# Layer 0's checks moved into bursts at the ends of rounds, and a new order in the first six pairs of the joint sums

## The chip, the cores and the metric

The kernel runs on one core of one Trainium2 chip. The core has five engines that run on their own queues and meet only at semaphores: TensorE (PE, matrix products into PSUM), VectorE (DVE), ScalarE (ACT), GpSimd (POOL) and SyncE (SP), which here only issues transfers. Transfers run on 16 DMA engines. The metric is the device time of one execution in microseconds; three runs of the kernel before took 573.9, 572.15 and 574.8 us, median 573.9.

## The reference, cut to what matters

Four graph layers follow each other on the same 4096 nodes with 64 features and one 4096 x 4096 adjacency matrix `adj` of zeros and ones:

```
h = relu(layernorm(x));  x = x + L0(h)   # att = adj * sigmoid(scores(q, k)); att @ h, normalised
h = relu(layernorm(x));  x = x + L1(h)   # weighted sum over the last 100 neighbours by rank, + bias
h = relu(layernorm(x));  x = x + L2(h)   # 1 - 0.1 h - 0.01 * rowsum(h * (adj @ h))
h = relu(layernorm(x));  x = x + L3(h)   # relu([h, adj @ h / degree] @ W.T)
```

Layer 0 needs a full 4096 x 4096 matrix of sigmoids, masked by `adj`, times a 4096 x 64 matrix. Layer 1 needs running counts of each row's neighbours. Layers 2 and 3 both need a product of `adj` with 64 columns, and are summed jointly in the kernel.

## The kernel before

`adj` stands in DRAM as f32, cut into 8 blocks `ib` of 512 rows and, in each block, 16 tiles `g` of 2 x 128 columns. GpSimd loads it once as FP8 masks that stay in SBUF (`load_masks`, L211). That is exact only where the entries are zeros and ones. So the kernel also reads `adj` again as f32 and lets VectorE test every entry; this is a check (`check`, L441 and L438 in its `fetch`). An accumulated count of odd entries goes into `odd`, and at the end a flag decides whether a general version of the model (`model(True)`) has to run. A check in layer 0 takes half a tile, 128 x 512 (tile `ck`, three buffers, `CHECKED`); later checks take a whole tile, 128 x 1024 (tile `ckw`, or free space of `s2a`). A check has no effect on the other work except that it takes VectorE's time, a transfer on SP's queue, and a buffer. `fetch` puts the transfer in front of its check in the program; SP runs ahead and issues it as soon as the buffer is free, that is when the check three before it has ended.

**Layer 0.** After a prologue up to about 58 us, the scores are made in rounds. A round has four tiles (the rounds of the first two blocks after the prologue's 18 tiles have 4, 4, 3 and 3), a block has four rounds. For each tile, TensorE makes the scores into one of three PSUM buffers of two banks (`scores`, L1059), ScalarE takes the sigmoid (`sigmoids`), and VectorE multiplies with the mask (`masked`). The first sigmoid of a round is written to SBUF and so frees its PSUM buffer by itself; the other three stay in PSUM, and VectorE's product frees the buffer. After the four tiles come, on TensorE, the sums with the four tiles of the round before (`gather`, L1090). When a block is complete, `rows0` is pushed onto a list of jobs: one part of it is emitted after each tile (`on`, which calls `step`). Its parts go TensorE (pt, L266), ScalarE, GpSimd (sup), ScalarE (sq), VectorE (inn, rs_y), GpSimd (a root by Newton steps, rs_a, then sup and x_sb), VectorE (st), GpSimd (xc), ScalarE (sq), VectorE (va, rs_y), GpSimd (the root again), VectorE (xc), GpSimd and VectorE (s2a, the input of layer 1). Each engine takes its instructions in the order in which the program emits them; no scheduler changes it (`manual_schedule`).

From the 33rd tile on, five of eight tiles are followed by a check, 60 in layer 0: after tiles with `k % 8` in (0, 2, 4, 5, 7), so one to three among the four products of a round. `taken`, between tile 84 and 112, issues copies of two mask rows per block on SP's queue (apart_m). If the number of checks left is odd after the loop, one more is made.

`Planned` wraps VectorE (`dve`) and ScalarE (`act`) and keeps a running estimate of when each will be done (`end`), from a cost of 0.07 us + 0.00105 us per column for VectorE. The planning of layer 1 uses it together with `clock`; in layer 0 `clock` stays at zero and nothing reads the estimates.

**Layer 1** first counts chunks (`many`), then runs rounds of four count products (L1500) and four sums (L1535), with checks by a plan: `due` grows in each round, and a check is made where the estimate says that VectorE is free.

**The joint sums** (`both_summed`) add up layers 2 and 3 for 32 tiles of 128 rows, in 16 pairs; a pair takes one PSUM bank, each tile 32 products over the chunks `t` (L1632), 1024 products in all. The last blocks of layer 1 are still being finished then by the jobs `rows1`: pr, then a norm, then ph (transposes, L1352), ht on ScalarE, pn (products, L1367), and the split into `s23`, which is what chunk `t` of the joint sums reads (`need` emits jobs until chunk `t` is ready). After every 8 products `beat` emits one part of each job, and every second beat a check. The first six pairs (`LEAD`) run side by side over the first 28 chunks (`SPLIT`): with `SKEW = 1`, pair `p` is `p` chunks behind pair 0. In `rows1` a number of empty parts stands in front of ph: 6 for blocks 6 and 7 (`late`), else 1; blocks 0 to 3 are `early`.

Of the kernel before, what the change touches and what calls it, by code (L numbers as in the profile page):

```python
# [28 lines left out]
IB = 512  # L29
# [49 lines left out]
def kernel(  # L79
# [87 lines left out]
    def model(general):  # L167
# [901 lines left out]
        def sigmoids(ps, to=None):  # L1069

            to = ps if to is None else to
            act.activation(to, ps, AF.Sigmoid, bias=att_c, scale=att_a)
            return to
# [119 lines left out]
        with tc.manual_schedule():  # L1193
            acc, late = first_rows_and_block()
            push(rows0(order0[0], evacuated(order0[0], acc, 0)), 10)
            pro_stack.close()
            mp1 = pool("mask_b", 1, side="right")
            for ib in order0[EARLY:]:
                get_mask(mp1, ib)
            spare.append(pool("pp1", 1, l0, space=PSUM))  # L1200
            if not general:
                push(count_constants(), 1)
            asking = iter(())

            def on():
                step()
                next(asking, None)

            sizes = [2] * 8 if general else [4] * 4
            first = [2] * 7 if general else [4, 4, 3, 3]
            sizes = first + (NIB - 2) * sizes + [0]
            k, done = NG + 2, NG
            LEAVING = {112 - 4 * ib: ib for ib in range(NIB)}
            for size in sizes:
                now = []
                for n, (ib, g) in enumerate(todo[k : k + size]):
                    edge[0] = n == size - 1
                    ps = scores(ib, g)  # L1220

                    if size > 2 and not now:
                        att = frm = sigmoids(ps, att_tile(ib, g))
                    else:
                        frm, att = sigmoids(ps), att_tile(ib, g)
                    masked(ib, g, frm, att)
                    now.append((ib, g, att))
                    load_masks(1)
                    k += 1
                    if k == 92 and not general:  # L1230
                        push(count_constants_2(), 1)
                    if not general and k in LEAVING:
                        taken(LEAVING[k])
                    if k > 2 * NG and k % 8 in (0, 2, 4, 5, 7):
                        check()
                    on()
                for ib, g, att in late:
                    at = done % NG
                    if at == 0:
                        acc = pa0.tile([P, IB], F32, tag="pa", name=f"acc0_{ib}{sfx}")  # L1240
                        if ib > 0:
                            asking = queries(ib - 1)
                    gather(acc, fb, g, att, at)
                    if at == NG - 1:
                        push(rows0(ib, evacuated(ib, acc, 0)), 10)
                    done += 1
                late = now
            edge[0] = True
            if len(checks) % 2:
                check()  # L1250
            if general:
                drain()
# [61 lines left out]
        def rows1(ib, asb):  # L1314
            tag = f"1_{ib}"
            rows = block(ib)
            xr = x_sb[:, rows, :]
            yield
            yield from claim("bank")
            pt = pm.tile([P, CI, D], F32, tag="pr", name=f"pr{tag}{sfx}")  # L1320
            for c in range(CI):
                nc.tensor.matmul(
                    pt[:, c, :], asb[:, c * P : (c + 1) * P], wln_sb[:, 0, :],
                    start=True, stop=True,
                )
            yield
            dve.tensor_tensor(xr, xr, pt, ALU.add)
            yield
            used.discard("bank")
            h = fa[:, rows, :]  # L1330
            if general:
                yield from norm(rows, h, tag, True)
                return
            early, late = ib < NIB - 4, ib >= NIB - 2
            yield from norm(rows, h, tag, True, kept=kept, pool=early)
            yield from split(h, s2b, rows)
            yield
            if early:
                nc.gpsimd.tensor_scalar(h, h, -0.1 / UP, None, ALU.mult)
                nc.gpsimd.tensor_tensor(h, h, xr, ALU.add)  # L1340
            else:
                dve.scalar_tensor_tensor(h, h, -0.1 / UP, xr, ALU.mult, ALU.add)
            yield
            scratch = s23[:, rows, 2:4, :].rearrange("p t k d -> p t (k d)").bitcast(F32)
            yield from norm(rows, h, f"3_{ib}", True, 1.0, late, h, sq=scratch, pool=early)
            for _ in range(6 if late else 1):
                yield
            yield from claim("rows")
            yield from claim("bank")
            pt = pm.tile([P, CI, P], F32, tag="pr", name=f"ph_{ib}")  # L1350
            for c in range(CI // 2):
                nc.tensor.transpose(  # L1352
                    pt[:, c, :], h[:, 2 * c : 2 * c + 2, :].rearrange("p c d -> p (c d)"), ident
                )
            yield
            ht = temps.tile([P, CI // 2, P], F32, tag="ht", name=f"ht_{ib}")
            act.copy(ht, pt[:, 0 : CI // 2, :])
            for _ in range(2 if late else 1):
                yield
            pn = [  # L1360
                pm.tile([P, CI // 2, 2, D], F32, tag="pr", name=f"pn_{ib}_0"),
                bank(turn_of_banks(), f"pn_{ib}_1", (P, CI // 2, 2, D)),
            ]
            v = temps.tile([P, CI, D], F32, tag="two", name=f"v2_{ib}")
            for c in range(CI):
                half = slice(c % 2 * D, (c % 2 + 1) * D)
                nc.tensor.matmul(  # L1367
                    pn[c % 2][:, c // 2, :, :].rearrange("p s d -> p (s d)"),
                    ht[half, c // 2, :],
                    wln_sb[half, 1:3, :].rearrange("p s d -> p (s d)"), start=True, stop=True,  # L1370
                )
            for n in (1, 0):
                act.copy(h[:, n::2, :], pn[n][:, :, 0, :])
                act.copy(v[:, n::2, :], pn[n][:, :, 1, :])
            yield
            used.discard("bank")
            yield from split(v, s23[:, :, 2:4, :], rows)
            used.discard("rows")
            ready.setdefault(2, set()).add(ib)
# [227 lines left out]
        if general:  # L1607
# [1 line left out]
            stream2 = pool("stream2", 2, l2)  # L1609
            own_sb = epi2.tile([P, NT, D], F32, name="own" + sfx)  # L1610
            v_sb3 = epi2.tile([P, NT, D], F32, name="v3" + sfx)
        SKEW = 1
        summed, beats = [0], [0]

        def beat():
# [296 lines left out]
```

## Time and profile before

One execution was profiled; its own time is 572.18 us, of which the recorded span is 569.5 us.

| | before |
|---|---|
| median of three runs | 573.9 us (572.15 to 574.8) |
| profiled execution, its span | 572.18 us, 569.5 us |
| granted TensorE clock, mean | 0.997 |
| busy: TensorE, VectorE, ScalarE, GpSimd | 552.0, 467.5, 358.8, 272.2 us |
| layer 0 after the prologue | 58 to 296 us |
| chunk counts, then layer 1 | 296 to 311 us, 311 to 444 us |
| joint sums | 444 to 563 us, the end at 569.5 |

Between 140 and 260 us VectorE is busy 36 to 37 us of every 40 and TensorE over 39 of 40; the 16 DMA engines are busy nearly all of the time there, most of it with the mask loads on GpSimd's queue, until about 250 us. From 482 to 556 us TensorE has no idle time.

How to read the rows: in a timeline the first number is the start in us from the span's start, the second the duration, then the engine, the line, the operation, the tile written and those read, and the count; brackets hold the idle time before the row and what ended it. In the list of waits the numbers are the total, the count and the longest. In the chain of waits each row is what held up the next one. L73 is the helper of `Planned`, so VectorE's and ScalarE's rows all carry it and are told apart by their tiles.

### The profile page before, as it was taken

What the parts mean: (1) busy time and instruction counts of PE and PEld (TensorE: products, weight loads), DVE (VectorE), ACT (ScalarE), POOL (GpSimd) and SP (SyncE); (2) the same over time, 40 slices, a digit from 0 to 9 for tenths busy, and PEclk for the clock granted to TensorE, in tenths of its full rate; (3) what the DMA queues carried; (4) which work ended last, traced back from release to release, by engine and by line L of the source; (5) the groups of instructions that cost most, each with busy time, mean ns of one, the idle gap of its engine ahead of it and who ended that gap; (6) DMA issues with size and microseconds to landing.
All of it is one profiled execution on the core that took longest, in us unless ns stands there. A gap on an engine that the chain in (4) does not pass through costs nothing.

```text
span 569.5 us, 9915 instructions
## 1 busy us (share of the span) xinstructions
PE 552.0 (97%) x3368; PEld 280.8 (49%) x3368; DVE 467.5 (82%) x949; ACT 358.8 (63%) x663; POOL 272.2 (48%) x526
## 2 busy tenths in 40 slices
PE   8999999999999999999999999999999999999995
PEld 3563333333333333333334444445454788888884
DVE  4679657799999999898976877778969897799993
ACT  3677667766676776778741888988888432342231
POOL 7624402675757576754444510384634343334332
PEclk9999999999999999999999999999999999999998
DMA  8995952689999999994223465453544788859960
GB/s 145 133 106 47 100 50 20 57 131 154 150 169 150 166 126 173 152 158 121 74 89 113 151 209 168 132 170 112 155 145 132 241 266 304 274 190 323 343 251 21
DMA packets 45612, 87.86 MB, mean 154 GB/s; under 512 B 6272, under 2 KB 24576, under 8 KB 45552
## 3 DMA queue, kind: packets, MB, share of 16 engines
q1 hardware_dynamic: 26112, 69.14, 36.5%
q0 software_dynamic: 18912, 17.77, 33.0%
q8 instruction: 28, 0.46, 0.3%
q10 hardware_dynamic: 528, 0.23, 0.2%
q14 instruction: 32, 0.26, 0.2%
HBM read 135.60 MB, written 1.05 MB: 240 GB/s over the span
## 4 chain that ended last, share of the span: by engine, by line
PE 70%; DVE 13%; POOL 5%; ACT 5%; issue 3%; DMA 2%; DVEq 0%; ACTq 0%; POOLq 0%; SPq 0%
PE acc L1090 15%; PE acc L1632 15%; PE ps L1059 15%; PE acc L1535 8%; PE cnt L1500 8%; PE idle L1183 3%; DVE att L73 3%; DVE ckw L73 2%; PE many L1387 1%; DMA s2a<-adjt_dram 1%; DVE s2a L73 1%; ACT ps L73 1%; DVE rrq L73 1%; POOL mask L211 1%; PE pt L266 1%
## 5 line engine op out<-in xcount | busy, mean ns | idle before, releaser
L1059 PE MATMUL ps<-qt,kt 64*128 64x512 f32 x512 | 123.4, 610 | 3.4 <-DVE att L73 3.0
L1090 PE MATMUL acc<-att,fb 128*64 128x512 f32 x512 | 117.8, 599 | 0.6 <-DVE att L73 0.5
L1632 PE MATMUL acc<-s,mask 128*128 128x256 f16 x1024 | 114.0, 273 | 0.4 <-DVE s L73 0.4
L73 ACT ACTIVATE w<-cnt 128x512 int16<-128x512 f32 x187 | 98.6, 606 | 12.1 <-PE cnt L1500 11.0
L1632 PEld LDWEIGHTS <-mask 128*128 128x128 fp8e4 x1024 | 99.8, 98 | 13.0 <-issue 1.0
L73 DVE TENSOR_TENSOR att<-ps,mask 128x1024 f32<-128x1024 f32 x82 | 98.6, 1217 | 8.6 <-ACT ps L73 8.5
L73 DVE SCALAR_TENSOR_TENSOR ckw<-ckw 128x1024 f32<-128x1024 f32 x76 | 96.0, 1274 | 4.2 <-DMA ckw<-adjt_dram 4.2
L73 ACT ACTIVATE ps<-ps,att_c,att_a 128x1024 f32<-128x1024 f32 x82 | 93.8, 1175 | 1.3 <-PE ps L1059 0.8
L73 ACT ACTIVATE att<-ps,att_c,att_a 128x1024 f32<-128x1024 f32 x46 | 54.6, 1202 | 54.1 <-PE ps L1059 53.9
L1059 PEld LDWEIGHTS ps<-qt,kt 64*128 64x128 f32 x512 | 44.8, 186 | 79.0 <-issue 28.7
L211 POOL DMA_DIRECT2D mask<-adjt_dram x128 | 70.1, 560 | 19.1 <-DMA mask<-adjt_dram 17.4
L73 DVE TENSOR_TENSOR att<-att,mask 128x1024 f32<-128x1024 f32 x46 | 56.9, 1252 | 18.8 <-ACT att L73 18.5
L1500 PE MATMUL cnt<-mask,after 128*128 128x512 fp8e4 x256 | 67.4, 379 | 2.7 <-DVE two L73 0.8
L1090 PEld LDWEIGHTS acc<-att,fb 128*64 128x64 f32 x512 | 33.5, 136 | 73.0 <-issue 67.6
L1535 PE MATMUL acc<-w,s2a 128*128 128x512 bf16 x256 | 66.2, 379 | 1.2 <-ACT asb L73 1.2
L73 DVE TENSOR_SCALAR w<-cnt 128x512 int16<-128x512 f32 x69 | 46.9, 686 | 22.6 <-PE cnt L1500 22.2
L301 POOL TENSOR_TENSOR rs_a<-rs_y 128x4 f32<-128x4 f32 x48 | 19.1, 398 | 67.4 <-DVE rs_y L73 61.0
L73 DVE SCALAR_TENSOR_TENSOR ck<-ck 128x512 f32<-128x512 f32 x60 | 42.8, 713 | 0.0
L1535 PEld LDWEIGHTS <-s2a 128*128 128x128 f16 x256 | 24.6, 98 | 33.6 <-issue 5.6
L1500 PEld LDWEIGHTS <-after 128*128 128x128 bf16 x256 | 24.4, 99 | 31.0 <-issue 2.7
L73 ACT ACTIVATE xm<-xm,inn 128x64 f32<-128x64 f32 x32 | 10.4, 347 | 45.9 <-DVE high L73 44.2
L1183 PE MATMUL idle<-ones 128*128 128x512 bf16 x126 | 30.9, 401 | 1.6 <-DVE ones L73 1.6
(248 smaller groups left out, 611.9 us busy)
## 6 DMA issues: line engine op xcount, KB each, us to landing
ckw<-adjt_dram SPq DMA_DIRECT2D x76, 512.0 KB, 4.3
mask<-adjt_dram POOLq DMA_DIRECT2D x128, 128.0 KB, 8.7
ck<-adjt_dram SPq DMA_DIRECT2D x60, 256.0 KB, 5.9
s2a<-adjt_dram SPq DMA_DIRECT2D x22, 512.0 KB, 4.9
x_sb<-x_dram SPq DMA_DIRECT2D x4, 256.0 KB, 7.5
out_dram<-y POOLq DMA_DIRECT2D x15, 64.0 KB, 3.7
apart_m<-mask SPq DMA_DIRECT2D x16, 16.0 KB, 4.1
mask<-apart_m SPq DMA_DIRECT2D x16, 16.0 KB, 4.3
```

Of the source, the lines that this page charges most:

```text
L73: return op(out, *args, **kw)
L211: nc.gpsimd.dma_start(out=masks[ib][:, g * CG : (g + 1) * CG, :], in_=adjt[ib, g])
L266: nc.tensor.transpose(pt[:, c, :], part, ident)
L301: nc.gpsimd.tensor_tensor(a, y, y, ALU.mult)
L1059: nc.tensor.matmul(ps[:, c, :], kt[half, g, :], qts[ib][half, :], start=True, stop=True)
L1090: nc.tensor.matmul(acc[c * D : (c + 1) * D, :], lhs[:, t, :], rhs[:, c, :], start=(at == 0), stop=(at == NG - 1), skip_group_check=True,)
L1183: nc.tensor.matmul(v.idle[:, v.filling % CG, :], ones, ones.unsqueeze(1).to_broadcast([P, IB // P, P]), start=True, stop=True, skip_group_ ...
L1387: nc.tensor.matmul(pc[q * NT : (q + 1) * NT, :], lane[:, NT - 1 - t : 2 * NT - 1 - t], masks[quad * QUAD + q][:, t, :], start=(t == 0), st ...
L1500: nc.tensor.matmul(cnt, by, what, start=True, stop=True, skip_group_check=True)
L1535: nc.tensor.matmul(accs[ib], apart_s if t < 0 else both(s2a, t), w, start=(t == NT - 1), stop=False, skip_group_check=True,)
L1632: nc.tensor.matmul(acc[:, to, :, :].rearrange("p k d -> p (k d)"), masks[ib][:, t, c * P : (c + 1) * P], s23[:, t, :, :].rearrange("p k d ...
```

## The change

Three places are touched. In layer 0 the check after a tile goes. Instead `clock` is set at the loop's start and grows by 7.7 for each round; a tile's product is planned no earlier than 2.1 + 1.2 n into its round; and after the products of a round, `due` grows by 2.5 (60 checks over 24 rounds) and checks are emitted while one is due and the plan says that VectorE would be done before the next round's first product, or three are due. The jobs of the round's tiles are emitted before the burst. As built, the bursts have 2 and 3 checks in turn, 60 in all as before.

In `rows1` the empty parts in front of ph become 5 for blocks 6 and 7, 3 for blocks 4 and 5, and stay 1 for blocks 0 to 3. `SKEW` becomes 0: the six pairs take each chunk together.

```diff
-            k, done = NG + 2, NG
+            k, done, due = NG + 2, NG, 0.0
+            TURN_0, FIRST_0, EACH_0, CHECKS_0 = 7.7, 2.1, 1.2, 60
+            clock[0] = max(dve.end, act.end)
...
+                    dve.end = max(dve.end, clock[0] + FIRST_0 + EACH_0 * n)
                     masked(ib, g, frm, att)
...
                     if not general and k in LEAVING:
                         taken(LEAVING[k])
-                    if k > 2 * NG and k % 8 in (0, 2, 4, 5, 7):
+                    on()
+                if k > 2 * NG and now:
+                    due += CHECKS_0 / (NIB - 2) / (NG / size)
+                    while due >= 1 and (
+                        dve.end + dve.cost(IB) < clock[0] + TURN_0 + FIRST_0 or due >= CHECKED
+                    ):
                         check()
-                    on()
+                        due -= 1
+                clock[0] += TURN_0
                 for ib, g, att in late:
...
-            for _ in range(6 if late else 1):
+            for _ in range(5 if late else 1 if early else 3):
                 yield
...
-        SKEW = 1
+        SKEW = 0
```

As built, the orders on TensorE and VectorE change where this says. Over layer 0 VectorE's row work keeps its place among the products, and a block reads, by VectorE's tiles: four products with va and rs_y before the last, two checks; two products, xc, two products, three checks; a product, s2a, three products, inn and rs_y, two checks; four products, st, three checks. On SP the apart_m copies stand up to three check transfers earlier. GpSimd's order is the same throughout, ScalarE's up to the joint sums.

## The prediction

> **What bounds the kernel now**
>
> Read in this order: the page, TensorE's waits, its timeline, the chain of work, VectorE's timeline beside it, and the landing of the checks' transfers. The page says that TensorE carries the kernel:
>
> ```profile
> span 569.5 us, 9915 instructions
> PE 552.0 (97%) x3368; PEld 280.8 (49%) x3368; DVE 467.5 (82%) x949; ACT 358.8 (63%) x663; POOL 272.2 (48%) x526
> ```
>
> Of the 17.5 us in which TensorE is idle, 3.3 lie in the first 60 us and 6.2 in the last 13.5 (windows); the change touches neither. Of its waits, these bear on the change, the first in layer 0, the others where the joint sums begin:
>
> ```profile
> PE ps L1059 <- DVE att L73: 3.0, 5, 0.8
> PE ph L1352 <- DVE x_sb L73: 0.5, 1, 0.5
> PE acc L1632 <- DVE s L73: 0.4, 1, 0.4
> ```
>
> Some loss hides in stretched rows. TensorE's timeline, start and duration first:
>
> ```profile
> 192.30 3.70 PE L1059 MATMUL ps<-qt,kt 64*128 64x512 f32 x16
> 195.93 3.65 PE L1090 MATMUL acc<-att,fb 128*64 128x512 f32 x16
> 199.52 3.92 PE L1059 MATMUL ps<-qt,kt 64*128 64x512 f32 x16
> 203.37 3.65 PE L1090 MATMUL acc<-att,fb 128*64 128x512 f32 x16
> 206.96 1.99 PE L1059 MATMUL ps<-qt,kt 64*128 64x512 f32 x8
> 209.56 1.99 PE L1059 MATMUL ps<-qt,kt 64*128 64x512 f32 x8 [0.62 <-DVE att L73]
> ```
>
> From start to start an undisturbed round is 3.63 of scores and 3.59 of sums. A round's third scores need the PSUM slot that the last product of the round before gives back, so that product's deadline is 1.83 us into the next round (half of 3.63 and the gap). It is missed once in a block of four rounds, and the chain of waits says why:
>
> ```profile
> 192.03 1.21 DVE att L73
> 195.13 1.05 POOL rs_a L301
> 199.65 1.09 POOL sup L1039
> 203.12 1.08 POOL mask L211 x2
> 205.20 1.17 ACT ps L73
> 206.39 1.22 DVE att L73
> 208.28 1.24 DVE att L73
> 209.56 1.99 PE ps L1059 x8
> ```
>
> VectorE reaches the row statistics late, so GpSimd's root and norm are late, ScalarE's square holds up the third sigmoid, and the last product misses its deadline. Checks stand in front of all this:
>
> ```profile
> 204.81 0.68 DVE L73 SCALAR_TENSOR_TENSOR ck<-ck 128x512 f32<-128x512 f32 x1
> 205.42 0.08 DVE L73 DVE_READ_ACCUMULATOR ck<-ck 128x1 f32 x1
> 206.39 1.22 DVE L73 TENSOR_TENSOR att<-ps,mask 128x1024 f32<-128x1024 f32 x1 [0.89 <-ACT ps L73]
> ```
>
> The answer on the tile ck says when a check's data is there, 5.9 us after the issue:
>
> ```profile
> DMA to landing us min/median/max: 2.6/5.9/7.9
> ```
>
> **The change, part by part**
>
> *What there is to win in layer 0.* In TensorE's timeline the four waits after the first check (178.62, 209.56, 240.88, 264.49) are 0.77, 0.62, 0.77 and 0.68: 2.84. Seven score rows (at 138.07, 145.60, 168.43, 199.52, 230.46, 237.90, 269.99) exceed 3.70, or 1.99 for half a row, by 0.20 to 0.32: 1.64. Together 4.48, the upper bound. The wait of 0.21 at 110.81 is before any check and stays.
>
> *The load.* Still 60 checks, 10 a block, now in bursts of 3 and 2 behind a round's products. VectorE's starts lie 1.14 apart behind a product and 0.61 behind a check; the row work of a block takes 1.11 (inn), 0.52 (st), 0.75 (va), 0.34 (xc) and 0.86 (s2a). So 16 x 1.14 + 10 x 0.61 + 3.58 = 27.9 us a block, against TensorE's 4 x 7.22 + 0.59 (pt) + 0.37 (pq) = 29.8. Starts of pt at 149.45, 180.54, 211.48, 242.80 and 273.82 give 30.9 to 31.3 now.
>
> *The new order by hand*, in the block shown. Third round: two checks no longer stand before inn, so the root's seed ends at 193.7, not 194.98, and GpSimd's chain begins 1.3 earlier. Fourth round: two checks to 194.9, then four products, the second at 197.3 behind its sigmoid; the last ends at 200.7. Deadline 199.52 + 1.83 = 201.35: the stretch of 0.22 goes. st to 201.2, three checks to 203.0. Next round: the first product starts at 203.0 (was 202.53), the third sigmoid ends 1.2 earlier, at 205.2; products at 203.0, 204.1 and 205.3, va to 207.2, the last product to 208.4, before the deadline of 208.79. The wait goes, with 0.2 to 0.4 to spare. Products here range from 1.21 to 1.64, so I leave 0.15 at each of five blocks: 0.75. Layer 0 gains 4.48 - 0.75 = 3.7; bounds 0 and 4.48, apart from late transfers.
>
> *The transfers, a new wait.* Three buffers: a check's transfer is issued when the check three before it ends. Today the tightest gap from issue to check is 6.6 us and no check waits (idle 0.0 in its group). In bursts, issues are 0.61 apart, and by the hand order the gap is 6.4 for the second check of a two-burst and the last of the three-burst behind it, 7.6 or more for most others. During mask loading, transfers issued 1.75 apart (179.20, 180.95) landed 2.1 apart by their packets (183.69, 185.79). So the second lands at 5.9 + 2.1 - 0.61 = 7.4, 1.0 late. Behind a waiting check stand the next round's four products, and behind these TensorE's scores; but that round's last product has 1.45 us to its deadline, and a block has 29.8 - 27.9 = 1.9 to spare. I take 0. From below the price is 0 (landing 5.9); from above, every queued transfer later than 7.4, priced in the third rival.
>
> The Trainium skill, "DMA: Bandwidth & Descriptors", section "Queues, rings and completion order", says that each DMA engine alternates between the queues that have work, one packet at a time. With GpSimd's mask queue always loaded, a check's transfer would move at half speed: 1.4 us alone (the transfer issued at 274.26 has packets from 0.95 to 2.31 us after its issue), so an estimated 2.8 instead of 2.1, the second landing 1.7 late, 0.25 over the slack, twice a block for 4.5 blocks: 2.2 less gain, and the sum would end at 571.6. The measured 2.1 decides.
>
> *Queues passed.* On SP the copies apart_m<-mask of the last block now stand before three check transfers instead of behind two of them; SP waited there until 258.64, so those start at 259.8 and land by 262.3 (2.5 without mask traffic), for a burst at 263.5. ScalarE and GpSimd keep their order, mask issues included. The final burst ends near 296.4 instead of 294.6; VectorE's next check waits for a transfer until 299.19. If its buffers come 0.4 later, wn_size is ready by 301.0, for TensorE at 301.20. Layer 1 keeps every engine's order and just moves.
>
> *Joint sums.* Same 1024 matmuls, 0.109 each start to start. Chunk 24 is first read after 288 instead of 258 of them, 3.3 us later, so the wait of 0.43 (a gap of 0.705, 0.60 over 0.109) goes. Block 5's transposes come 8 matmuls later, 0.87; what they wait for, x_sb at 457.61, ends at 458.02: 0.58 goes. Pair 5's bank is taken after 10 instead of 40 matmuls, at 445.2; its reader asb ends by 444.7. Block 6 goes the other way: its pn would start at 472.7, but ht ends at 472.95 on ScalarE, behind block 7's root, and a check (1.14) now stands before block 7's kept sum, which with VectorE's order costs some 0.2. A new wait of 0.4. Net 1.18 - 0.4 = 0.8; bounds 0 (that check delays all behind it) and 1.2. VectorE is busy 35.48 of 36 us from 520 to 556, but its run starts behind ScalarE's high at 489.32 after 1.57 idle and so moves along.
>
> *Sum.* -3.7 - 0.8 = -4.5. The profiled execution took 572.18 us (span 569.5 and 2.7 around it), so 567.7. It lies 1.7 below the median of the three runs, 573.9; against that, 569.4.
>
> **The rivals**
>
> 1. The forecast, 569.4; its own range 568 to 571.
> 2. GpSimd, not VectorE's checks, sets the third sigmoid: five mask issues (2.72 us) stand between x_sb and the norm whatever VectorE does. For it: its spans vary from 0.2 to 1.07 for the same rs_a. Against: the chain enters it from VectorE. Then the stretches go, the waits halve and the joint sums give 0.5: -1.6 - 0.5, 571.8.
> 3. Slower: bursts choke on their own transfers. VectorE's spare 1.9 us a block must be eaten first; beyond it each microsecond is TensorE's, over 4.5 blocks under mask loads. To end 2.9 above 573.9 it takes (4.5 + 2.9) / 4.5 = 1.65 more, 3.6 us of waiting a block: five queued transfers landing 0.7 beyond their gaps of 6.4 to 7.9, so at about 8 on average. Single ones reach 7.9 today, the median is 5.9. Then 577.
> 4. The wins are taken back, say by the flag's matmul at 556.05 waiting for VectorE, or late transfers that just use them up: 573.5.
>
> **How the numbers follow**
>
> Chances 0.62, 0.20, 0.12 and 0.06. A measurement of this kernel tells about 0.5% (2.9 us) from no change: the line is 571.0. Faster: the forecast and a little of rival 2, 0.66; same 0.22; slower 0.12. The range begins at both upper bounds off the lowest run, 572.15 - 4.48 - 1.2 = 566.4, and ends at 573.8, above rivals 2 and 4; what is out is rival 3 and a little.
>
> **What would show it**
>
> Right: TensorE's waits on att in layer 0 shrink from 3.0 to under 1.2, pt starts 29.8 to 30.1 apart, no DMA row before ck above 2 us in all, ph without its wait, pn with one below 0.5. Wrong: idle of ck <- DMA of 3 us a block, a third sigmoid still near 5.7 us into its round, or new waits past 460.

## The result, and where the time went

The changed kernel takes 575.64 us at the median of 17 runs (573.97 to 577.53), the kernel before 573.16 in the 17 runs beside it. The ratio is 1.0040, with a 95% interval of 1.0024 to 1.0056: 2.3 us slower. That is inside the band of 0.5% that the prediction counted as no change, but the interval leaves 1 out, so the small loss is real. The forecast was 569.4, its range 566.4 to 573.8. It missed, on the slow side.

The page of the profiled execution after the change (574.75 us, span 573.2) begins:

```profile
span 573.2 us, 9901 instructions
PE 551.2 (96%) x3356; PEld 280.7 (49%) x3368; DVE 472.2 (82%) x949; ACT 358.7 (63%) x663; POOL 267.1 (47%) x526
```

VectorE is 4.7 us busier than before, although it runs the same 949 instructions. TensorE's waits (us in total, times, longest) are now:

```profile
PE ps L1059 <- DVE att L73: 4.4, 8, 0.8
PE cnt L1509 <- DMA mask<-two: 1.5, 1, 1.5
PE pn L1376 <- ACT ht L73: 1.1, 1, 1.1
```

The first was to fall from 3.0 to under 1.2. The second was 0.4 before. The third is the new wait that the forecast put at 0.4; the waits of ph and of the joint sums' acc are gone, as it said. VectorE's own waits between 100 and 300 us begin with one that was not there at all before, the checks' wait for their transfers:

```profile
DVE ck L73 <- DMA ck<-adjt_dram: 6.8, 7, 1.4
DVE att L73 <- ACT att L73: 3.1, 4, 1.4
DVE att L73 <- ACT ps L73: 2.6, 5, 1.4
DVE st L73 <- POOL x_sb L1040: 2.2, 4, 0.7
```

And the checks themselves took longer. This is their group in the page of before, then in that of after (busy time, mean ns of one, idle time in front):

```profile
L73 DVE SCALAR_TENSOR_TENSOR ck<-ck 128x512 f32<-128x512 f32 x60 | 42.8, 713 | 0.0
```

```profile
L73 DVE SCALAR_TENSOR_TENSOR ck<-ck 128x512 f32<-128x512 f32 x60 | 44.7, 781 | 6.8 <-DMA ck<-adjt_dram 6.8
```

TensorE's timeline of the block that the prediction worked through has the missed deadline still in its place, with a second wait in front of it:

```profile
200.43 3.70 PE L1059 MATMUL ps<-qt,kt 64*128 64x512 f32 x16
204.06 3.65 PE L1090 MATMUL acc<-att,fb 128*64 128x512 f32 x16
208.04 2.26 PE L1059 MATMUL ps<-qt,kt 64*128 64x512 f32 x8 [0.32 <-DVE att L73]
211.07 1.99 PE L1059 MATMUL ps<-qt,kt 64*128 64x512 f32 x8 [0.77 <-DVE att L73]
```

The chain of work through this block no longer passes through GpSimd, ScalarE's sigmoid and their square. From the burst on it is VectorE alone:

```profile
204.29 1.02 DVE ck L73 x2
205.30 3.81 DVE att L73 x3
209.11 0.34 DVE va L73
...
209.79 1.24 DVE att L73
...
211.07 1.98 PE ps L1059 x7
```

VectorE's timeline of the same stretch, and GpSimd's row beside it, say what the burst met:

```profile
202.45 0.42 DVE L73 TENSOR_REDUCE st<-x_sb 128x4 f32<-128x256 f32 x1 [0.70 <-POOL x_sb L1040]
...
203.59 0.69 DVE L73 SCALAR_TENSOR_TENSOR ck<-ck 128x512 f32<-128x512 f32 x1
...
204.21 1.09 DVE L73 SCALAR_TENSOR_TENSOR ck<-ck 128x512 f32<-128x512 f32 x1
...
205.23 1.62 DVE L73 TENSOR_TENSOR att<-att,mask 128x1024 f32<-128x1024 f32 x1
...
209.79 1.23 DVE L73 TENSOR_TENSOR att<-ps,mask 128x1024 f32<-128x1024 f32 x1
```

```profile
205.06 0.70 POOL L332 TENSOR_TENSOR xc<-x_sb,st 128x256 f32<-128x256 f32 x1
```

st comes late, the three checks stand behind it, the third check (1.09, not 0.69) and the next product (1.62, not 1.22) run beside GpSimd's xc, and the round's last product ends at 211.02, 2.98 us into its round against a deadline of 1.83.

By stages: layer 0, from the first scores of the tenth tile (at 63.65 us before; the prologue's 18 tiles are scored until 79.6 us, not 58) to the first `many` matmul, takes 234.2 us instead of 232.2. The counting matmul behind it waits 1.1 longer for its transfer, and the joint sums, from their first to their last matmul, take 0.2 less. So the loss is in layer 0, where the gain was forecast.

### The profile page after: what moved, and what is told of

Same layout as the page of the kernel before. It is cut to its first block, busy times and chain, and to the rows that moved or that the text cites. A ratio compares the mean times of both kernels' runs of the same rounds, so it can differ in the third digit from the quotient of the medians.

```text
span 573.2 us, 9901 instructions
## 1 busy us (share of the span) xinstructions
PE 551.2 (96%) x3356; PEld 280.7 (49%) x3368; DVE 472.2 (82%) x949; ACT 358.7 (63%) x663; POOL 267.1 (47%) x526
## 4 chain that ended last, share of the span: by engine, by line
PE 65%; DVE 17%; ACT 5%; POOL 5%; DMA 4%; issue 3%; ACTq 0%; DVEq 0%; POOLq 0%; SPq 0%
PE acc L1641 15%; PE ps L1059 14%; PE acc L1090 13%; PE cnt L1509 8%; PE acc L1544 8%; DVE att L73 8%; PE many L1396 1%; DVE ckw L73 1%; DMA s2a<-adjt_dram 1%; DMA vec<-vecs_dram 1%; DMA mask<-adjt_dram 1%; ACT w L73 1%; DMA mask<-two 1%; PE idle L1183 1%; DVE rrq L73 1%
## 5 line engine op out<-in xcount | busy, mean ns | idle before, releaser
L73 DVE TENSOR_TENSOR att<-ps,mask 128x1024 f32<-128x1024 f32 x82 | 96.8, 1215 | 3.5 <-ACT ps L73 2.9
L73 DVE TENSOR_TENSOR att<-att,mask 128x1024 f32<-128x1024 f32 x46 | 59.4, 1306 | 15.1 <-ACT att L73 15.1
L1544 PE MATMUL acc<-w,s2a 128*128 128x512 bf16 x244 | 64.1, 379 | 1.8 <-ACT asb L73 1.2
L73 DVE SCALAR_TENSOR_TENSOR ck<-ck 128x512 f32<-128x512 f32 x60 | 44.7, 781 | 6.8 <-DMA ck<-adjt_dram 6.8
L301 POOL TENSOR_TENSOR rs_a<-rs_y 128x4 f32<-128x4 f32 x48 | 15.8, 330 | 70.7 <-DVE rs_y L73 64.3
```

Source lines behind the costliest of these rows:

```text
L73: return op(out, *args, **kw)
L301: nc.gpsimd.tensor_tensor(a, y, y, ALU.mult)
L1544: nc.tensor.matmul(accs[ib], apart_s if t < 0 else both(s2a, t), w, start=(t == NT - 1), stop=False, skip_group_check=True,)
```

## The experiments

Three theories were set against each other. *Theory 1*: the bursts wait for their own transfers. *Theory 2*: it is the order, a burst of three behind a late st and in front of the next round's first product. *Theory 3*: VectorE is full, because its rows beside GpSimd's cost more than the forecast charged.

Each run was timed beside the kernel before. In the table, "rows" is what VectorE's rows occupy in a block of four rounds: the mean length of five blocks (between the starts of pt) less the idle time that VectorE's timeline shows in front of its rows. The two waits are TensorE's on att and VectorE's on a check's transfer, in us, over the whole execution. These columns and layer 0 come from one profiled execution of each run. Runs with the same code in layer 0 show how far that can be trusted: before and joint alone differ by 0.1 us, the whole change and layer 0 alone by 0.5.

```
run                          ratio to before [95%]      layer 0   rows   att    ck
before                       1                          232.2     28.6   3.0    0
the whole change             1.0040 [1.0024, 1.0056]    234.2     29.4   4.4    6.8
layer 0 alone                1.0044 [1.0022, 1.0065]    233.7     29.3   4.4    5.1
joint sums alone             0.9981 [0.9959, 1.0002]    232.3     28.6   3.1    0
no transfers                 0.9998 [0.9978, 1.0017]    232.2     29.7   4.0    0
burst before the jobs        1.0079 [1.0049, 1.0109]    237.6     29.5   8.1    4.0
other phase                  1.0040 [1.0021, 1.0060]    234.0     29.2   5.0    3.8
other phase, no transfers    0.9994 [0.9977, 1.0011]    231.8     29.5   3.4    0
no checks                    0.9910 [0.9880, 0.9941]    227.7     22.7   0.5    -
moved check                  1.0056 [1.0032, 1.0079]    235.7     29.4   5.7    2.0
four buffers                 0.9993 [0.9972, 1.0013]    231.2     29.1   3.1    0
three buffers                1.0027 [1.0013, 1.0041]    233.2     29.2   4.1    5.1
eight a block, spread        1.0043 [1.0027, 1.0058]    234.3     27.5   4.0    0
eight a block, bursts        1.0012 [0.9997, 1.0027]    233.8     28.0   3.9    1.5
short checks, no transfers   0.9944 [0.9918, 0.9969]    229.4     27.8   0.9    0
no bias row, no transfers    0.9989 [0.9972, 1.0006]    231.9     28.9   3.8    0
48 in layer 0, bursts        0.9935 [0.9911, 0.9960]    229.4     28.0   1.3    0.9
36 in layer 0, bursts        1.0003 [0.9981, 1.0024]    228.7     26.9   0.5    0
48, none behind st           0.9951 [0.9931, 0.9971]    230.4     28.1   2.5    1.1
48, spread                   0.9960 [0.9934, 0.9985]    231.0     27.6   1.9    0
```

**Each part alone.** The first run takes back the joint sums' two edits, the second takes back layer 0's.

```diff
-            for _ in range(5 if late else 1 if early else 3):
+            for _ in range(6 if late else 1):
-        SKEW = 0
+        SKEW = 1
```

> Layer 0's bursts as in the changed kernel; the joint sums as before. If layer 0 carries the whole loss (its mark at the first matmul of `many` came 1.75 us later, the counting matmul behind it 2.85 later), this run ends 2.0 to 3.1 us above the kernel before, near 575.8, and the row `DVE ck <- DMA ck<-adjt_dram` shows 5 to 8 us again. If the joint sums carry it, this run is at most 0.5 us above the kernel before.

> The joint sums as in the changed kernel; layer 0 as before. By the traces: the waits of ph (0.5) and acc (0.4) go, a wait of pn on ht of about 1 us comes, net -0.2 us, within 0.1% of the kernel before. By the prediction's step: -0.8 us, pn waiting 0.4. The wait `cnt <- DMA mask<-two`, 0.4 before and 1.5 after, stays at 0.4 if layer 0's bursts made it 1.1 longer, and is anything from 0.4 to 1.5 if it is chance.

Layer 0 alone is 0.44% slower, as much as the whole change; the joint sums alone are 0.19% faster, with an interval that just reaches 1. So layer 0 carries the loss. The wait `cnt <- DMA mask<-two` is 1.1 in the second run, whose layer 0 is that of before, and between 0.4 and 1.5 in the others, 0.4 again in the run with bursts and no transfers: the 1.1 us more in the profile of after can't be put down to the bursts. The joint sums' pn waits 0.8 for ht in their run:

```profile
PE cnt L1500 <- DMA mask<-two: 1.1, 1, 1.1
PE pn L1367 <- ACT ht L73: 0.8, 1, 0.8
```

**Without the transfers.** Checks from the fourth on read the three tiles that are already there.

```diff
-                at = ck.tile([P, IB], F32, tag="ck", name=f"ck_{k}", bufs=CHECKED)
-                nc.sync.dma_start(out=at, in_=adjt[ib, t // CG][:, t % CG, :])
+                if k < CHECKED:
+                    at = ck.tile(...)
+                    nc.sync.dma_start(...)
+                    stays.append(at)
+                at = stays[k % CHECKED]
```

> As the run of layer 0 alone, but layer 0's checks from the fourth on read the three tiles that are already loaded: 57 transfers of 256 KB are left out, and with them the check of most of layer 0's half of the matrix. Theory 1 (the bursts' waits for their own transfers, 6.8 us, make VectorE late): the wait ck<-DMA is 0, TensorE's wait on att falls from 4.4 to under 1.5, layer 0 ends 3 to 4 us earlier than before, total near 569.5 to 571. Theory 2 (the order: a burst of three behind a late st, in front of the next round's first product): the wait ck<-DMA is 0 but TensorE's wait on att stays at 3 to 4.5 and the total within 1.2 us of layer 0 alone, 574 to 576.

The answer lies between. By the ratios to before, the time falls by 0.46%, 2.6 us (the medians, 576.9 and 573.74 us, lie 3.2 apart); in the profiles layer 0 is 1.5 us shorter. So the waits for transfers cost some 1.5 to 2.6 us. But layer 0 is then just as long as before: nothing of the forecast's 3.7 appears, and TensorE still waits for att:

```profile
PE ps L1062 <- DVE att L73: 4.0, 7, 0.8
```

VectorE's timeline of this run, the burst behind the round of pt and the product after it, and GpSimd's beside it:

```profile
185.41 1.02 DVE L73 SCALAR_TENSOR_TENSOR ck<-ck 128x512 f32<-128x512 f32 x1
...
186.36 0.68 DVE L73 SCALAR_TENSOR_TENSOR ck<-ck 128x512 f32<-128x512 f32 x1
...
186.97 1.26 DVE L73 SCALAR_TENSOR_TENSOR ck<-ck 128x512 f32<-128x512 f32 x1
...
188.16 1.83 DVE L73 TENSOR_TENSOR att<-att,mask 128x1024 f32<-128x1024 f32 x1
```

```profile
184.97 0.91 POOL L286 TENSOR_SCALAR s2a<-xc 128x256 f16<-128x256 f32 x1
185.77 1.15 POOL L211 DMA_DIRECT2D mask<-adjt_dram  x2
186.90 0.78 POOL L1052 TENSOR_TENSOR x_sb<-x_sb,vec 128x256 f32<-128x256 f32 x1
187.58 0.57 POOL L211 DMA_DIRECT2D mask<-adjt_dram  x1
188.17 0.74 POOL L280 TENSOR_TENSOR sup<-asb 128x256 f32<-128x256 f32 x1
```

The check at 186.36 stands beside mask issues but for its last 0.14 us and takes 0.68; those at 201.84 and 202.45, beside mask issues alone, take 0.69. The two that overlap a row of 256 elements for longer take 1.02 and 1.26, and the product beside sup takes 1.83. Over the five blocks, split by whether a VectorE row overlaps such a row of GpSimd by more than 0.1 us: in this run 31 checks stand alone and take 0.685 on average, 19 stand beside and take 1.005; of the products that read att from SBUF, 12 alone take 1.220 and 8 beside 1.601; products that read the sigmoid from PSUM take 1.215 alone and 1.218 beside. In the kernel before, 13 checks stand beside, at 0.778. What the rows beside GpSimd's take more closes the sum: 19 times 0.32 and 8 times 0.38 over five blocks are 1.8 us a block, and the forecast's 27.9 and 1.8 are 29.7. The split has a weakness: GpSimd's recorded times are rough, and four of the 19 checks (like the one at 203.06, beside a row recorded at 203.91) overlap a row only because they are long. A run below takes a row away instead.

**The phase of the bursts.** The plan begins half a check ahead, so bursts of three become two and the reverse.

```diff
-            k, done, due = NG + 2, NG, 0.0
+            k, done, due = NG + 2, NG, 0.5
```

> As the run of layer 0 alone, but the plan begins half a check ahead, so that bursts of two and three change places: three behind inn and behind va, two behind st and behind the xc product of the root. Theory 2 (a burst of three between st and the next round's first product is what misses the deadline): the first product of that round starts 0.7 earlier or more, TensorE's wait on att falls to 3 us or less, total 1.5 to 3 us under layer 0 alone. Theory 3 (VectorE is full, since checks and first products beside GpSimd's rows of 256 elements take 1.0 and 1.6 us and not 0.68 and 1.22): the wait only moves; VectorE's idle time stays under 10 us over five blocks, total within 1.2 us of layer 0 alone. Theory 1: ck<-DMA stays at 5 us or more in either case.

> The same change of places without the transfers (checks from the fourth on read the three tiles already loaded; the check of most of layer 0's half of the matrix is left out). Theory 2: TensorE's wait on att, 4.0 without transfers, falls under 1.5, and the total to 570.5 to 572. Theory 3: the wait stays between 3 and 4.5 and the total within 1 us of the run without transfers (573.7).

Theory 2 wanted 1.5 to 3 us; the two runs gain 0.04% each on their counterparts, within their intervals. TensorE's waits only move, as theory 3 has it. The checks' wait for transfers fell to 3.8 us where 5 or more was expected of theory 1, and nothing was gained by it.

**The burst in front of the last tile's jobs.** The round's last step of the queue of jobs comes behind the burst.

```diff
-                    on()
+                    if n < size - 1:
+                        on()
...
+                if now:
+                    on()
```

> As the run of layer 0 alone, but a burst stands ahead of the last turn of the queue of jobs in its round, so VectorE's st or s2a of that turn comes behind the burst and not in front of it. Theory 2: the waits of st on x_sb (2.2 us in 4) shrink below 0.5 and no check stands behind them; TensorE's wait on att falls by 1 to 2 us, total 1 to 2 us under layer 0 alone. Theory 1: ck<-DMA stays at 5 us or more, and the total within 0.7 us of layer 0 alone.

The waits of st on x_sb did go, and it is the slowest run of all: inn and st now stand behind the checks, and everything that hangs on them comes later. The order that theory 2 blamed was the better one.

**What there was to win.** All of layer 0's checks are left out.

```diff
-                        check()
+                        if checks:
+                            checks.popleft()
```

> As the run of layer 0 alone with none of layer 0's 60 checks, neither transfers nor VectorE's work: that half of the check of the matrix is left out. It measures what there was to win in layer 0, put at 4.48 us: if VectorE's checks cause all of TensorE's waits on att there, the wait is 0, block periods are 29.8 and the total is near 569.1. If GpSimd's mask issues in front of xc set the third sigmoid whatever VectorE does, the waits shrink only to half, 1.5 to 2 us, and the total is near 571.5.

Layer 0 is 4.5 us shorter than before, and TensorE's wait is down to this:

```profile
PE ps L1059 <- DVE att L73: 0.5, 2, 0.3
```

The upper bound of 4.48 was right, and so was its cause: GpSimd's mask issues are all still there.

**The forecast's lesson applied by hand.** The order of before, with the check in front of inn moved behind the first product of the round after st, where VectorE waits 0.89.

```diff
-                    if k > 2 * NG and k % 8 in (0, 2, 4, 5, 7):
+                    if k > 2 * NG and k % 16 in (0, 1, 2, 4, 5, 7, 8, 10, 13, 15):
```

> The joint sums as in the changed kernel; layer 0 in the order of before, but for one check in a block: the one in front of inn stands behind the first product of the round after st, in VectorE's wait of 0.89 there. Theory 3 (only rows that overlap GpSimd's are dear, and the chain of inn, root, x_sb, xc, third sigmoid sets the last product): the root's seed comes 0.6 earlier, checks stay at 0.71 on average, ck<-DMA at 0 to 1, TensorE's wait on att falls from 3.0 to 1 or less, the total to 569.5 to 571.5 (1 to 3 under the joint sums alone). If the mask issues set the third sigmoid by themselves, the wait stays above 2 and the total within 0.7 of the joint sums alone, 572.7.

It missed: 0.75% above the joint sums alone. The root's seed did come 0.6 earlier (196.05 in a round that starts at 193.97). But the moved check met GpSimd's xc: it took 1.13, and the wait that was to hide it was gone. GpSimd's xc also began 0.6 us earlier in its round, so the sigmoid behind it came earlier too.

```profile
204.21 1.23 DVE L73 TENSOR_TENSOR att<-att,mask 128x1024 f32<-128x1024 f32 x1
205.36 1.13 DVE L73 SCALAR_TENSOR_TENSOR ck<-ck 128x512 f32<-128x512 f32 x1
...
212.07 0.69 DVE L73 SCALAR_TENSOR_TENSOR ck<-ck 128x512 f32<-128x512 f32 x1 [0.80 <-DMA ck<-adjt_dram]
```

**A fourth buffer.** Only 480 of 512 columns are loaded and checked, since so a fourth tile fits.

```diff
-                at = ck.tile([P, IB], F32, tag="ck", name=f"ck_{k}", bufs=CHECKED)
-                nc.sync.dma_start(out=at, in_=adjt[ib, t // CG][:, t % CG, :])
+                at = ck.tile([P, 480], F32, tag="ck", name=f"ck_{k}", bufs=BUFFERS)
+                nc.sync.dma_start(out=at, in_=adjt[ib, t // CG][:, t % CG, 0:480])
```

> As the run of layer 0 alone (its bursts), with checks and transfers of 480 of a chunk's 512 columns (32 columns of each are left unchecked, since only so a fourth buffer fits) and four buffers in place of three. Theory 1 with its cause in the buffers: each transfer is issued one check earlier, ck<-DMA falls below 1.5 us and the total 1 to 2.5 us below the same with three buffers. If the transfer engines are simply full, the wait stays above 3 us and the total within 0.7 us of three buffers.

> The control of the run before: 480 columns, three buffers. Checks take 0.64 in place of 0.68 us and transfers move 6% less, so ck<-DMA stays at 3.5 to 6 us and the total is 575 to 576.5, at most 1 us below layer 0 alone.

The control came out 0.5 us below what was expected of it, at 574.52. From three buffers to four the wait ck<-DMA goes from 5.1 to 0, layer 0 is 2.0 shorter and the median 1.7 lower. The landing times do not change; this is the answer on ck with four buffers, then with three:

```profile
DMA to landing us min/median/max: 2.6/6.1/9.7
```

```profile
DMA to landing us min/median/max: 2.6/6.0/9.7
```

So what the bursts lack is lead, not speed. The profiled execution of four buffers is the longest of its twelve (576.12 us, median 572.86); it loses part of the gain again in the joint sums, told below.

**Fewer checks, twelve of them early.** Eight a block, and the twelve that this frees behind the products of tiles 19 to 30; spread in the order of before, and in bursts of two.

```diff
-                    if k > 2 * NG and k % 8 in (0, 2, 4, 5, 7):
+                    if k <= 30 or (k > 2 * NG and k % 16 in (0, 4, 5, 7, 8, 10, 13, 15)):
```

```diff
-            TURN_0, FIRST_0, EACH_0, CHECKS_0 = 7.7, 2.1, 1.2, 60
+            TURN_0, FIRST_0, EACH_0, CHECKS_0 = 7.7, 2.1, 1.2, 48
...
+                    if k <= 30:
+                        check()
                     on()
```

> The joint sums as in the changed kernel; layer 0 in the order of before with 8 checks a block in place of 10 (none in front of inn, none between the second and the third product of the round after st), and the 12 that this takes out behind the products of the first rounds (tiles 19 to 30), where VectorE waits 0.3 to 3.1 us for ScalarE. Theory 3 (VectorE's load in the two rounds of inn and st makes the last product late): TensorE's wait on att falls from 3.0 to 0.5 to 1.5, the total to 569.5 to 571.5. If what counts is the total of VectorE's and GpSimd's meetings anywhere, or the early checks delay the first rounds, the total is 572 to 574.

> The whole change with 8 checks a block, in bursts of two, and the same 12 checks early. If the load is what decides (29.7 of 29.8 us a block with ten checks, so some 28 with eight), the order by bursts does as well as the spread one: TensorE's wait on att below 1.5, ck<-DMA below 3, total 569.5 to 571.5. If bursts are bad in themselves (meetings with GpSimd's rows, late transfers), the wait stays above 2.5 and the total is 1.5 us or more above the spread order with eight a block.

Both missed, in the part that was argued from idle time: from the first start of pt to the second it is now 35.7 (spread) and 35.9 us (bursts) and not 32.4, with these waits in the run with bursts:

```profile
91.78 1.99 PE L1059 MATMUL ps<-qt,kt 64*128 64x512 f32 x8 [0.61 <-DVE att L73]
...
113.71 1.13 PE L1059 MATMUL ps<-qt,kt 64*128 64x512 f32 x4 [1.22 <-DVE att L73]
```

Behind 122 us the five blocks are 2.0 (bursts) and 1.2 (spread) shorter than before's. And where bursts were to be 1.5 us worse if they are bad in themselves, they are 0.31% better.

**The load that the forecast charged.** No transfers, and checks cut to 360 columns.

```diff
+                if made[0] >= CHECKED and tiles == 1:
+                    at = at[:, 0:360]
```

> As the run without transfers, with layer 0's checks cut to 360 of 512 columns from the fourth on (the check of layer 0's half of the matrix is left out but for three tiles, as there). The rows then cost VectorE about what the forecast charged: 29.7 less ten times 0.17 is 28 us a block, in the same order and beside the same rows of GpSimd. If the load decides, TensorE's wait on att falls from 4.0 to under 1.5 and the total by 2 to 3.5 us, to 570 to 571.5. If GpSimd's root and mask issues set the last product whatever VectorE's load is, the wait stays above 2.5 and the total within 1 us of 573.5.

In the same order, with 27.8 us of rows to a block, TensorE's wait falls to 0.9 and the time to 570.73 us, 0.56% under before:

```profile
PE ps L1064 <- DVE att L73: 0.9, 3, 0.3
```

This is theory 3's test, and it holds: the hand order gains most of what it promised (layer 0 is 2.8 us shorter than before, of 3.7) once the rows cost what it charged and no transfer is waited for.

**One row of GpSimd taken away.**

```diff
-            nc.gpsimd.tensor_tensor(
-                x_sb[:, rows, :], x_sb[:, rows, :], over_rows(bias1, CI), ALU.add
-            )
```

> As the run without transfers, and the row x_sb<-x_sb,vec of GpSimd (0.78 us, 128x256, once a block) is left out, so layer 0's output lacks one bias. If a row of GpSimd beside a burst stretches VectorE's, the check that stood beside it (1.26 us at 186.97) goes back to 0.68, checks beside GpSimd become fewer, VectorE has 0.5 us less a block, and the total falls by 1 to 2.5 us. If not, the check stays above 1 us there and the total within 0.7 us of 573.5.

The checks of that burst, at the place of the 1.02, 0.68 and 1.26 above, and what came of the time:

```profile
185.25 0.68 DVE L73 SCALAR_TENSOR_TENSOR ck<-ck 128x512 f32<-128x512 f32 x1
...
185.86 0.69 DVE L73 SCALAR_TENSOR_TENSOR ck<-ck 128x512 f32<-128x512 f32 x1
...
186.47 0.69 DVE L73 SCALAR_TENSOR_TENSOR ck<-ck 128x512 f32<-128x512 f32 x1
...
187.37 1.23 DVE L73 TENSOR_TENSOR att<-att,mask 128x1024 f32<-128x1024 f32 x1 [0.20 <-ACT att L73]
```

```profile
184.82 0.90 POOL L286 TENSOR_SCALAR s2a<-xc 128x256 f16<-128x256 f32 x1
...
187.89 1.28 POOL L280 TENSOR_TENSOR sup<-asb 128x256 f32<-128x256 f32 x1 [0.60 <-ACT asb L73]
```

With that one row the stretches of both checks and of the product behind them are gone, so GpSimd's rows do cause them. Recorded overlap does not say which row: s2a begins 0.43 us ahead of the first check in both runs, and that check takes 1.02 in one and 0.68 in the other. Order counts too: sup now begins 0.52 us into the product, and sup is the longer one (1.28 us, not 0.74) while the product takes 1.23. The time gains only 0.1%, within the interval, where 1 to 2.5 us were expected. VectorE had 0.8 us less a block and waited 0.7 us longer for ScalarE. Five of TensorE's six waits behind 120 us stand where they stood without transfers, 28.8 to 29.4 us behind the start of pt, where the last product of the round behind st is late. So VectorE's total in a block is not all that counts: 28.9 us of rows left a wait of 3.8 here, because the relief came in another round.

**Fewer checks, the rest in layer 1.**

```diff
-            TURN_0, FIRST_0, EACH_0, CHECKS_0 = 7.7, 2.1, 1.2, 60
+            TURN_0, FIRST_0, EACH_0, CHECKS_0 = 7.7, 2.1, 1.2, 48
-        PRODUCT, ROUND, CHECKS_1 = 0.216, 1.85, 35
+        PRODUCT, ROUND, CHECKS_1 = 0.216, 1.85, 41
```

> The whole change with 48 checks in layer 0 in place of 60, in bursts of two, and six checks of two chunks more in layer 1, where VectorE waits 22 us for TensorE's counts. By the run with eight a block and twelve early ones, layer 0 gains 2 us on before from its second block on; with the joint sums 570 to 572, if layer 1 takes the six for nothing; 573 to 575 if layer 1 pays for them.

> The same with 36 checks in layer 0 (six a block) and twelve of two chunks more in layer 1. By load alone VectorE has some 26 to 27 us of rows to a block of 29.8: TensorE's wait on att under 1 us, layer 0 3 to 4 us shorter than before, 569 to 571 if layer 1 takes the twelve for nothing; 572 to 576 if layer 1's counts wait for them.

With 48 the whole change takes 569.93 us: 0.65% less than before, and so faster than both kernels of this case. Layer 0 is 2.8 shorter, and from the first `many` matmul to the joint sums it takes 147.9 us as against 148.2, so layer 1 takes the six checks for nothing: there VectorE's wait for counts shrinks from 22.2 to 16.3.

```profile
PE ps L1059 <- DVE att L73: 1.3, 4, 0.6
```

```profile
DVE w L73 <- PE cnt L1509: 16.3, 19, 2.2
```

With 36, layer 0 gains 0.8 more, but that stretch of layer 1 takes 153.0 us: TensorE's counts now wait for ScalarE's w (1.5, before 0.7) and its sums for VectorE's:

```profile
PE cnt L1509 <- ACT w L73: 1.5, 2, 1.1
PE acc L1544 <- DVE w L73: 1.4, 2, 1.2
```

**Place or load.** The run with 48 without a burst behind st, so 3, 3, 2 and 0 in a block; and 48 in the spread order of before.

```diff
-                    due += CHECKS_0 / (NIB - 2) / (NG / size)
+                    due += CHECKS_0 / (NIB - 2) / 3 if k % NG else 0.0
```

```diff
-                    if k > 2 * NG and k % 8 in (0, 2, 4, 5, 7):
+                    if k > 2 * NG and k % 8 in (0, 2, 5, 7):
```

> As the run with 48 checks in layer 0 and six of two chunks more in layer 1, with no burst behind st: bursts of 3, 3, 2 and 0 in the four rounds of a block. If it is the round behind st whose rows count (a first product that starts late and beside GpSimd's xc), TensorE's wait on att falls from 1.3 to under 0.6, blocks from 30.4 to 30.1 us, total 0.5 to 1.5 us under the 569.9 of the run with 48. If only VectorE's total load counts, nothing changes (569.5 to 570.5); if bursts of three in two rounds running wait for their transfers, ck<-DMA is 3 us or more and the total 571 to 573.

> The kernel before with the joint sums of the change, 48 checks in layer 0 spread as before (none behind the fourth product of the round of inn), and six of two chunks more in layer 1. If the load alone decides, the same as 48 in bursts: TensorE's wait on att 1 to 1.5 us, total 569.5 to 570.5. If bursts are worse in themselves, this is 1 us or more below them, 567.5 to 569; if they are better, 571 to 572.5.

Taking the burst away from the one place that theory 2 named did not help (a wait of 2.5 against 1.3, and layer 0 is 0.9 longer, in a profiled execution that is the longest of its twelve for its joint sums). The spread order, at 571.54 us, lies where it was expected if bursts are the better order, but the intervals of the two overlap. Theory 2 falls. What is left unsettled is a difference of 0.9 to 1.6 us in layer 0 between orders of the same load: the load decides most of the wait, the order some.

## Why the prediction was wrong, point by point

- **The upper bound of 4.48 in layer 0**: right, 4.5 measured without checks. Rival 2, that GpSimd's mask issues set the third sigmoid whatever VectorE does, falls with the same run.
- **"The load", 27.9 us a block**: this is the term that failed. It charged every check 0.61 and every product 1.14 from start to start, the durations of rows that stand alone. The order of the change makes it 29.7 (no transfers), with 29.8 of TensorE's work. The stretched rows were in the profile of before, where VectorE's rows took 28.6 a block, and the prediction quoted one-off products of up to 1.64; it left 0.15 a block for them and did not ask which of the moved rows would stand beside GpSimd's. Without transfers, checks of 360 columns bring the rows back to 27.8 and TensorE's wait from 4.0 to 0.9.
- **"The new order by hand"**: its steps came in the order told, later each time. Into their own rounds: the seed at 1.4 forecast, 2.2 without transfers, 3.0 in the changed kernel; the first product behind st at 3.5, 4.2 and 4.8; the last product's end at 1.4, 2.8 and 3.0, against the deadline of 1.83. The "0.2 to 0.4 to spare" were smaller than the stretch of one check.
- **"The transfers", costed at 0**: wrong by about 2 us (2.6 by the run without transfers, 1.7 by the fourth buffer). In the two-burst of the changed kernel from 179.62 to 182.16 the transfers of 171.90 and 172.52, the ends of the checks three before, were waited for until 179.62 and 181.54: 7.7 and 9.0 us, where the forecast had 5.9 and 7.4. The spacing of 1.9 is near the 2.1 that it used, partly by luck: the pair from which it read 2.1 landed 1.0 apart (issued at 179.20 and 180.95, landed after 5.95 and 5.18 us), for 183.69 is where half of the two transfers' packets had ended, not where the first had landed. It was the first of the two that came late, and its "1.9 us to spare" in a block rested on the 27.9 of the step above. Why that first transfer was late, by the mask loads beside it or by its place in its queue, no run separates.
- **The Trainium skill, "DMA: Bandwidth & Descriptors", section "Queues, rings and completion order"**: by its alternation between queues the forecast estimated 2.8 us a transfer and 571.6 in all. That section says that each DMA engine goes round the queues that have work, a packet from each in turn. The spacing of 1.9 us between the two landings does not show the 2.8 at that place, and both sums erred at the landing of the first, 7.7 us.
- **Rival 3, slower by late transfers**: the right mechanism, at 1.4 us of waiting a block (6.8 over five blocks), not 3.6. It began to cost earlier than the rival said, because by the measured rows VectorE had 0.1 us to spare and not 1.9.
- **The joint sums, 0.8**: not contradicted, but not shown. Alone they gain 0.19% (1.1 us, between 2.4 and a loss of 0.1); beside the bursts, the whole change is 0.04% better than layer 0 alone; in the profiles the stretch from their first to their last matmul is 0.2 and 0.4 us shorter. The waits of ph and acc went as forecast; pn waits 0.8 to 1.1 in place of the 0.4 forecast.
- **Queues passed, at 0**: nothing in the runs speaks against it.

Together: of the 3.7 forecast for layer 0 the stretched rows took all, late transfers added some 2 to 2.6, and the joint sums gave 0.2 to 1.1 back. That makes 0.9 to 2.4 us more than before, where the whole change measured 2.3 (1.4 to 3.2); the parts' own intervals are some 1.2 us each way.

## What to carry to other kernels

When rows are moved by a plan of an engine's load, charge each row by what it will stand beside, not by its mean or its best: here a check cost 0.68 alone and 1.0 beside GpSimd's tensor rows, and the forecast's slack was smaller than that difference. A burst of transfers needs as many buffers as give the last of it the lead that the first had; three that sufficed for spread checks fell 2 us short for bursts. And when an engine is within a few per cent of the bound in one stage, moving work to a stage where it waits (48 checks in layer 0, six double ones in layer 1) gave more than any order within the full stage.

## What the runs showed of the hardware that was not expected

In these runs VectorE's rows were longer beside GpSimd's only where both their operands lie in SBUF. In the run without transfers: checks 0.685 alone and 1.005 beside, SBUF products 1.220 and 1.601 (the longest 2.33 in the run with the other phase), products that read PSUM 1.215 and 1.218. It goes both ways: GpSimd's small rows of the root take 0.20 us alone and 0.72 on average beside such rows (85 and 30 of them without transfers). GpSimd's mask issues alone did not stretch a check. The Trainium skill, "SBUF — State Buffer", section "Who interferes with whom", says that a VectorE instruction with two SBUF inputs contends with a GpSimd instruction that reads SBUF, and that one with at most one SBUF input does not, outside the 2-port modes. These means agree with it; single rows do not always, as the check beside s2a shows that took 0.68 without the bias row.

The joint sums are not equally long in profiles of kernels whose joint sums are the same program: from 118.5 to 123.5 us in the ten runs that have them as before. VectorE's y waits for the transfer out of an earlier y, and in the profiles where it waits longest the flag's matmul waits for VectorE, for up to 2.9 us. Before, y waits 3.4 and the flag's matmul not at all; with four buffers:

```profile
DVE y L73 <- DMA out_dram<-y: 6.0, 4, 3.1
```

```profile
PE pf L1306 <- DVE bad L73: 2.9, 1, 2.9
```

This hides part of the gain in that run's profile, whose layer 0 was 2.0 shorter than with three buffers. That the one wait causes the other is not shown: no run tested it.
